# Deformable layer of a four-layer kernel: block end, first sample and one norm re-ordered

## The chip, the cores and the metric

The kernel runs on one core of a Trainium2 chip. Its engines work side by side, each through its own instructions in order: TensorE (PE) multiplies matrices, VectorE (DVE) and ScalarE (ACT) work elementwise, GpSimd (POOL) does elementwise work too, and SyncE (SP) issues most of the DMAs. The metric is the device time of one execution in microseconds (us), of which the median over several runs is given.

## The reference

The input x is fp32, 8 samples of 384 channels on a 32 x 32 image. Four layers follow each other, each as `x = x + layer(groupnorm(x))`:

```python
x = x + L0(_gn(x), ...)   # selective state-space scan (Mamba), 32 groups in _gn
x = x + L1(_gn(x), ...)   # deformable convolution, this case's main subject
x = x + L2(_gn(x), ...)   # layer norm, selective scan, MLP
x = x + L3(_gn(x), ...)   # shifts and a 5 x 5 filter per shift group
```

Layer 1 splits the channels into three groups of 128, one for each kernel size K = 3, 5, 7:

```python
def deform_block(x, ow, ob, dw, pw, pb, K):
    offsets = conv2d(x, ow, ob, K // 2)          # 2*K*K offsets per pixel
    out = deform_depthwise(x, offsets, dw, K, K // 2)
    return conv2d(out, pw, pb, 0)                # 128 -> 128, 1 x 1
...
out = jnp.concatenate([out3, out5, out7], axis=1)
return out * se_weight(out, fc1_w, fc2_w)        # squeeze and excite
```

`deform_depthwise` samples x at each tap's position plus its offset, bilinearly and with zeros outside the image, and sums over the K x K taps with one weight per channel and tap.

## The kernel before

Layer 0 and layer 2 are built by one function, in steps of two half samples; each step is a plan of units in which loads, products, scans and norms are put by hand. At the last step of layer 0 there is no next pair of samples, so `plan` puts in the norm of the deformable layer's first sample instead: `norm_load` (a DMA of x), `norm_stats` (DVE, L308), the aggregate (DVE, L146), the group mean (PE, L155), the deviations, their squares and sums, and the reciprocal root (ACT). Before the change this chain began at unit 0 of that step, as in all steps.

The deformable layer is `deform_fast`, from 2798.7 us to about 5260 us. A general version stands behind a flag for offsets out of reach. Bilinear weights are "hats": for the row distance (`hats_y`, two parts) and the column distance (`hats_x`), each an ACT absolute value and an ACT relu. DVE weighs the input cells with the tap weights (`weigh`, L1738, fxk) and multiplies the hats (`product`, L1755, fsm); PE multiplies fxk by fsm and accumulates in PSUM (`products`, L1792, wacc). Cells come from `cells_map` (DVE), `rows_pe` (PE transposes), `rows_act` (ACT), a store to DRAM (`cells_out`, fxd) and four loads that repeat them over partitions (`cells_in`, fxt8, 1 MB each). The positions (pixel plus offset) are stored (fposd) and read back repeated by `positions` (fpyx, 1 MB each).

A sample is three blocks, K = 3, 5, 7 (g = 0, 1, 2). A block is a list of units: its taps in groups of eight (four units each), and before them one single tap (two units). That makes 6, 14 and 26 units, 46 a sample. The loop in `deform_fast` runs over slots u: it issues the position load, then the work put in places act0, pe0 and dve0, then PE's unit u interleaved with DVE's unit u+1, then the hats due in this slot (y hats first), then act1, dve1 and pe1. Nothing reorders this: engines take instructions in the order issued. All tiles are rings of a fixed number of buffers, fhy 2, fhx 2, fpyx 2, fsm 6, fxk 4, fxt8 4, fw 4.

The accumulator has one buffer of five PSUM banks. So at a block's end, slot `end`, `sums_act` (act0, ACT copies fdsb<-wacc, L1474) and `sums` (dve0, L1479) empty it before PE starts the next block; `point`, `point_act` and, after K=7, the squeeze and excite follow in the next slots.

The offsets of K=3 and K=5 are direct convolutions on PE (`conv`, L1395). Those of K=7 are built from 16 pieces of short filters (`fir`, L1333), whose weights are computed once on POOL (`fir_weights`, firw), stored (fwd, on POOL's queue) and loaded piece by piece (`fir_load`, fw, on SP's queue). Pieces start five slots ahead of a sample, or three ahead for the first.

The first sample's x (xn0, tile fxn, 1.5 MB) is loaded in one DMA when layer 0 ends. Then per K: biases, a grid, weights; L1104 adds obk to the grid on POOL for K=7, and L1105 adds ob to obk on DVE for all K.

The lines of the profile that the change touches: L725 to L738 (norm), L1078 (load of xn0), L1104 and L1105, L1141 to L1152 (lead and hats), L1174 (act0), L1584 to L1589 (cells).

Of the kernel before, what the change touches and what calls it, by code (L numbers as in the profile page):

```python
# [10 lines left out]
ALU = mybir.AluOpType  # L11
# [6 lines left out]
G = C // P  # L18
# [84 lines left out]
class Net:  # L103
# [112 lines left out]
    def ssm_layer(self, li, src, dst, shift=None):  # L216
        tc, nc, ins = self.tc, self.nc, self.ins
# [4 lines left out]
        with ExitStack() as ctx:  # L222
# [455 lines left out]
            for b in range(self.nb):  # L678
                s0, s1 = {"b": b, "h": 0, "sl": slice(0, TS)}, {"b": b, "h": 1, "sl": slice(TS, L)}
# [13 lines left out]
            def plan(prev, s, nxt):  # L693
                act, dve, pool, pe = queues = [[[] for _ in range(T + NU)] for _ in range(4)]

                def put(q, t, fn, *args):
                    if not args or args[0]:
                        q[t].append((fn, *args))

                for j in range(ND):  # L700
                    t = NU * j
# [6 lines left out]
                    n, k = (s, j + 2) if j + 2 < ND else (nxt, j + 2 - ND)  # L708
# [13 lines left out]
                for t in sorted({*TG, *TS2}):  # L722
                    put(act, t, exp_ln)
                nn = nxt if nxt or mlp else {"b": 0, "h": 0, "src": dst}
                put(pe, 0, norm_load, nn)  # L725
                if nn and nn["h"] == 0:
                    put(dve, 2, norm_stats, nn, 0)
                    put(dve, 3, norm_stats, nn, 1)
                    put(dve, 3, lambda n: n.update(gn_mv=self.gn_aggr(n["gn_st"])), nn)
                    put(pe, 4, lambda n: n.update(gn_ps=self.gn_mean(n["gn_mv"])), nn)  # L730
                    put(dve, 5, lambda n: n.update(gn_grp=self.gn_dev(n["gn_mv"], n["gn_ps"])), nn)
                    put(act, 6, lambda n: n.update(gn_dm=self.gn_square(n["gn_grp"][1])), nn)
                    put(pe, 6, lambda n: n.update(gn_ps=self.gn_mean2(n["gn_dm"])), nn)
                    put(dve, 8, lambda n: n.update(gn_var=self.gn_sum(n["gn_grp"][0], n["gn_ps"])), nn)
                    to = () if nxt else self.gns[1]
                    put(act, 9, lambda n: n.update(gn=self.gn_rstd(n["gn_grp"][0], n["gn_var"], *to)), nn)
                    put(act, 9, lambda n: n["sib"].update(gn=n["gn"]), nxt)
                put(act, 10, norm_apply, nxt)  # L738
                if mlp:
# [52 lines left out]
            with tc.manual_schedule(engines=ENGINES):  # L792
# [40 lines left out]
                for i, (s, j, m) in enumerate(units):  # L833
                    c, t = divmod(i, T)
                    if t == 0:
                        queues = plan(
                            steps[c - 1] if c else None, s, steps[c + 1] if c + 1 < len(steps) else None
                        )
                        for k, q in enumerate(over or ()):
                            for i0, items in enumerate(q):  # L840
                                queues[k][i0][:0] = items
                        act, dve, pool, pe = queues
                        over = [q[T:] for q in queues]
# [228 lines left out]
    def deform_fast(self, src, dst):  # L1072
        tc, nc, ins = self.tc, self.nc, self.ins
        with ExitStack() as ctx:
            wp = ctx.enter_context(tc.tile_pool(name="w1f", bufs=1))
            self.q1 = ctx.enter_context(tc.tile_pool(name="q1", bufs=1))
            self.xn0 = self.q1.tile([P, G, L], F32, name="fxn")
            nc.sync.dma_start(out=self.xn0, in_=src(0))  # L1078
            self.fwd = self.dram.tile([P, NFIR * NFIR, 2 * 49], F32, name="fwd", bufs=1)
            with tc.tile_pool(name="fw", bufs=1) as fw:  # L1080
                self.fir_weights(fw.tile([P, NFIR, NFIR, 2 * 49], F32, name="firw"), ins["owf"])
# [4 lines left out]
            for g, K in enumerate(KS):  # L1086
                K2, (n, st, cols) = K * K, CONV[K]
                rows = 2 * K2
                queue = nc.scalar if K == 7 else nc.sync
                ow = None if n == 1 else wp.tile([P, K2, st], F32, name=f"fow{K}")  # L1090
                ob = wp.tile([P, 1], F32, name=f"fob{K}")
                obk = wp.tile([P, 1], F32, name=f"fobk{K}")
                grid = wp.tile([P, cols], F32, name=f"fgrid{K}")
                for t in (ob, obk, grid) + ((ow,) if n > 1 else ()):
                    nc.gpsimd.memset(t, 0.0)
                if n > 1:
                    queue.dma_start(out=ow[:, :, :rows], in_=ins[f"ow{K}"])
                for i in range(n):
                    r = slice(i * st, i * st + rows)
                    queue.dma_start(out=ob[r], in_=ins[f"ob{K}"])  # L1100
                    queue.dma_start(out=obk[r], in_=ins["c_cols"][:rows, Q_K + g : Q_K + g + 1])
                    queue.dma_start(out=grid[r], in_=ins["c_grid"][:rows, i * cols : (i + 1) * cols])
                if n == 1:
                    nc.gpsimd.tensor_scalar(grid[:rows], grid[:rows], obk[:rows], None, ALU.add)  # L1104
                nc.vector.tensor_tensor(obk, obk, ob, ALU.add)  # L1105
                nq = K2 // NO
                wk = wp.tile([P, nq + 1, P], F32, name=f"fwk{K}")
                for t in range(NO):
                    queue.dma_start(
                        out=wk[t::NO, :nq, :],  # L1110
                        in_=ins[f"dw{K}"][t : NO * nq : NO, :].partition_broadcast(CELL),
                    )
                queue.dma_start(out=wk[:, nq, :], in_=ins[f"dw{K}"][NO * nq, :].partition_broadcast(P))
                self.f[K] = (ow, ob, obk, grid, wk)
# [22 lines left out]
            for b in range(self.nb):  # L1137
                for g in range(G):
                    first[b, g] = len(units)
                    units += [(b, g, j, h) for j in self.order(g) for h in range(self.parts(g, j))]  # L1140
            hats, loads = {}, {}  # L1141
            for u, (b, g, j, h) in enumerate(units):
                if h == 0:
                    one = self.parts(g, j) == 2
                    lead = 4 if j == 0 else 3
                    loads[u - 5 if one or j else u - 6] = b, g, j
                    for t, fn, k in (
                        ((-3, self.hats_x, 0), (-2, self.hats_y, 0), (-1, self.hats_y, 1))
                        if one
                        else ((-lead, self.hats_x, 0), (-2, self.hats_y, 0), (-1, self.hats_y, 1), (0, self.hats_x, 1))  # L1150
                    ):
                        hats.setdefault(u + t, []).append((fn, b, g, j, k))  # L1152
            self.state = {}
            for b in range(self.nb):
                for g in range(G):
# [3 lines left out]
            def run(u, *where):  # L1159
                for place in where:  # L1160
                    for fn, *args in places.pop((u, place), ()):
                        fn(*args)

            engines = ENGINES - {mybir.EngineType.Pool}
            with tc.manual_schedule(engines=engines):
                for u in range(min(slots), max(slots) + 1):

                    def unit(i):
                        return units[i] if 0 <= i < len(units) else None

                    now, after = unit(u), unit(u + 1)
                    if u in loads:
                        self.positions(*loads[u])
                    run(u, "act0", "pe0", "dve0")  # L1174
                    if now and u == first[now[:2]]:
                        self.begin(now)
                    pe = list(self.unit_pe(*now)) if now else []
                    dve = list(self.unit_dve(*after)) if after else []
                    for k in range(max(len(pe), len(dve))):
                        for q in (pe, dve):  # L1180
                            if k < len(q):
                                q[k]()
                    for fn, *args in sorted(hats.get(u, ()), key=lambda h: h[0] == self.hats_x):
                        fn(*args)
                    run(u, "act1", "dve1", "pe1")
# [40 lines left out]
    def block_steps(self, b, g, first, put, weights, src, dst):  # L1226
        nc, K = self.nc, KS[g]
        K2, pad = K * K, K // 2
        n, st, cols = CONV[K]
        ow, ob, obk, grid, _ = self.f[K]  # L1230
# [5 lines left out]
        s0 = first[b, g]  # L1236
# [315 lines left out]
        if g == 0:  # L1552
            t = t0 - 30
# [19 lines left out]
        else:  # L1573
            t = t0 - 5 if b else t0 - 3
# [6 lines left out]
                    k += 1  # L1581
                put(t + k, "dve0" if ph > 1 else "act0", fir_take, ph)
            put(t + k, "dve0", fir_end)
        put(s0 - 5, "dve1", cells_map)  # L1584
        put(s0 - 4, "pe1", rows_pe)
        put(s0 - 3, "act0", rows_act)
        put(s0 - 3, "act0", cells_out)
        for q in range(4):
            put(s0 - 2 + q, "dve0", cells_in, q)  # L1589
        put(end, "act0", sums_act)  # L1590
        put(end, "dve0", sums)
        put(end + 1, "pe1", point)
# [544 lines left out]
```

## Time and profile before

| what | us |
|---|---|
| median of 3 runs | 8797.08 (8791.13 to 8799.9) |
| the profiled execution | 8793.49 |
| its span, first to last instruction | 8791.7 |
| deformable layer | about 2798.7 to 5260 |
| one sample of it, in the steady state | 297.3 |

The granted TensorE clock was 0.909 of full speed on average over the span. Busy time over the whole span (share and number of instructions):

```profile
PE 7389.6 (84%) x29688; PEld 3814.4 (43%) x29688; DVE 7510.6 (85%) x8477; ACT 5818.7 (66%) x9501; POOL 5571.8 (63%) x3383
```

PEld is the loading of weights into the array, which overlaps PE. No engine is full over the whole; each layer has its own limit. The slices show it (40 equal slices of the span, busy tenths):

```profile
PE   7888888788886899999999975788888888888886
...
DVE  6999999999996788988898886898898988898872
...
POOL 6999999999997000000000007999898989999954
```

In the eleven slices where POOL is at 0 the deformable layer runs: there PE is at 8 or 9 and DVE at 7 to 9.

### The profile page before, as it was taken

Reading aid. Unit: us, or ns where it says so; the run is one execution under the profiler, and the core shown is the slowest. Engines: PE = TensorE matmul, PEld = TensorE weight load, DVE = VectorE, ACT = ScalarE, POOL = GpSimd, SP = SyncE. Lnnn points to the kernel's source line nnn. Section 1 sums busy time; section 2 is a strip of 40 time slices with the busy share of each in tenths; the row PEclk is TensorE's granted clock in tenths of the full one; section 3 lists DMA queues with packets and bytes.
Section 4 is the critical chain, followed back from the end, with each engine's and each line's share of the span. In section 5 each row is a group of like instructions: output and inputs, shape, how many; then the busy total and the mean of one; then the engine's idle time right before and its main releaser. Section 6 shows DMA issues by size and latency. Waiting matters only on the chain. (4 is left out here: it accounts for less than half of the span.)

```text
span 8791.7 us, 91535 instructions
## 1 busy us (share of the span) xinstructions
PE 7389.6 (84%) x29688; PEld 3814.4 (43%) x29688; DVE 7510.6 (85%) x8477; ACT 5818.7 (66%) x9501; POOL 5571.8 (63%) x3383
## 2 busy tenths in 40 slices
PE   7888888788886899999999975788888888888886
PEld 2232233223222788788878861233333333333232
DVE  6999999999996788988898886898898988898872
ACT  6777777777774656665666556676777777776740
POOL 6999999999997000000000007999898989999954
PEclk8899899899887999999999997899889999999988
DMA  4555545555454654464446434566666656666646
GB/s 127 123 127 120 125 116 125 126 122 126 115 126 115 169 141 117 112 165 132 118 125 160 128 85 113 136 149 159 156 148 145 154 139 154 151 150 160 159 135 112
DMA packets 803572, 1179.30 MB, mean 134 GB/s; under 512 B 267042, under 2 KB 419650, under 8 KB 769288
## 3 DMA queue, kind: packets, MB, share of 16 engines
q1 hardware_dynamic: 743780, 1157.20, 53.7%
q10 hardware_dynamic: 57844, 10.06, 0.6%
q0 software_dynamic: 1456, 6.07, 0.2%
q8 instruction: 237, 3.88, 0.2%
q14 instruction: 255, 2.09, 0.1%
HBM read 984.11 MB, written 188.98 MB: 133 GB/s over the span
## 5 line engine op out<-in xcount | busy, mean ns | idle before, releaser
L539 POOL TENSOR_TENSOR db<-dub,bc 128x1024 f32<-128x1024 f32 x1536 | 3608.7, 2359 | 377.5 <-DVE hs L551 166.7
L531 ACT ACTIVATE da<-dtb,vec 128x512 f32<-128x512 f32 x3072 | 2122.1, 691 | 609.2 <-DVE hs L564 410.5
L551 DVE TENSOR_TENSOR_SCAN da<-da,db 128x1024 f32<-128x1024 f32 x960 | 2193.3, 2285 | 129.9 <-ACT da L531 86.9
L472 POOL TENSOR_TENSOR dt<-dt,sp_e 128x512 f32<-128x512 f32 x96 | 122.5, 1276 | 2473.1 <-DMA bc<-bcd 2468.8
L1792 PE MATMUL wacc<-fsm,fxk 128*128 128x195 f32 (+21 forms) x10624 | 1572.4, 306 | 132.5 <-DVE fsm L1755 69.7
L1792 PEld LDWEIGHTS wacc<-fsm,fxk 128*128 128x128 f32 x10624 | 1472.7, 195 | 269.1 <-DVE fsm L1755 141.3
L551 DVE TENSOR_TENSOR_SCAN hs<-da,db 128x1024 f32<-128x1024 f32 x576 | 1315.0, 2283 | 198.2 <-POOL db L524 86.2
L562 POOL TENSOR_TENSOR hs<-hs,bc 128x1024 f32<-128x1024 f32 x576 | 1358.0, 2358 | 33.8 <-ACT st L557 33.8
L564 DVE TENSOR_TENSOR hs<-da,bc 128x1024 f32<-128x1024 f32 x960 | 1175.5, 1224 | 127.9 <-PE y L574 78.6
L574 PE MATMUL y<-hs,cols 128*32 128x512 f32 x6144 | 975.4, 654 | 279.1 <-POOL hs L562 253.7
L1755 DVE TENSOR_TENSOR fsm<-fhy,fhx 128x585 f32<-128x585 f32 (+39 forms) x3136 | 1007.6, 383 | 92.9 <-PE wacc L1792 89.9
L1738 DVE TENSOR_TENSOR fxk<-fxt,fwk 128x1024 f32<-128x1024 f32 (+1 forms) x688 | 809.6, 1177 | 12.2 <-DMA fxt<-fxd 11.4
L1715 ACT ACTIVATE fhy<-fpyx,cell 128x416 f32<-128x416 f32 (+10 forms) x832 | 422.8, 580 | 374.7 <-DVE fsm L1755 374.6
L574 PEld LDWEIGHTS y<-hs,cols 128*32 128x32 f32 x6144 | 191.7, 114 | 1004.1 <-issue 516.1
L651 PE MATMUL ps_m<-hid,wm 128*128 128x512 f32 x1152 | 550.6, 633 | 61.8 <-ACT hid L646 27.8
L632 PE MATMUL ps_h<-t,wm 128*128 128x512 f32 x1152 | 531.1, 605 | 45.0 <-DVE sp_e L464 24.4
L1698 ACT ACTIVATE fhx<-fpyx,cell 128x352 f32<-128x352 f32 (+9 forms) x640 | 344.3, 609 | 237.0 <-DVE fsm L1755 222.8
L364 PE MATMUL ps_in<-xn,winr 128*128 128x512 f32 x576 | 326.8, 714 | 175.0 <-ACT xn L353 127.1
L651 PEld LDWEIGHTS ps_m<-hid,wm 128*128 128x128 f32 x1152 | 227.0, 203 | 394.7 <-issue 283.0
L632 PEld LDWEIGHTS ps_h<-t,wm 128*128 128x128 f32 x1152 | 216.1, 193 | 364.7 <-issue 273.4
L583 PE MATMUL ps_z<-xn,winr 128*128 128x512 f32 x576 | 303.0, 674 | 47.7 <-DVE sp_e L464 47.7
L1720 ACT ACTIVATE fhy<-fhy,cols 128x1184 f32<-128x1184 f32 (+8 forms) x208 | 307.4, 1478 | 6.8
(238 smaller groups left out, 9826.3 us busy)
## 6 DMA issues: line engine op xcount, KB each, us to landing
dtb<-dtd SPq DMA_DIRECT2D x768, 256.0 KB
dub<-dtd SPq DMA_DIRECT2D x768, 256.0 KB
fpyx<-fposd SPq DMA_DIRECT2D x104, 1024.0 KB
fxt<-fxd SPq DMA_DIRECT2D x96, 1024.0 KB
wm<-in_w SPq DMA_DIRECT2D x96, 768.0 KB
bc<-bcd SPq DMA_DIRECT2D x256, 256.0 KB
x<-x SPq DMA_DIRECT2D x73, 768.0 KB
dtd<-dt SPq DMA_DIRECT2D x192, 256.0 KB
```

Source lines behind the costliest of these rows:

```text
L531: nc.scalar.activation(da[:, i, :], s["dtb", j][:, k, :], AF.Exp, scale=na[:, j, n + i : n + i + 1])
L539: nc.gpsimd.tensor_tensor(db, du, s["bc"][p][:, 0], ALU.mult)
L551: nc.vector.tensor_tensor_scan(h1, da1, db1, 0.0, ALU.mult, ALU.add)
L562: nc.gpsimd.tensor_tensor(s["hs", m], s["hs", m], c, ALU.mult)
L564: nc.vector.tensor_tensor(hs_tile(s, m), s["da", m], c, ALU.mult)
L574: nc.tensor.matmul(s["y"][k * IP : (k + 1) * IP, :], sel, s["hs", p * NSUB + k][:, i, :], start=mlp and p == 0 and i == 0, stop=p == NQP - ...
L632: nc.tensor.matmul(ps, s["w1", q][:, k, f * P : (f + 1) * P], s["t"][:, k, :], start=(k == 0), stop=(k == G - 1))
L651: nc.tensor.matmul(ps, s["w2", q][:, f, o * P : (o + 1) * P], s["hid", q][:, f, :], start=(f == 0), stop=(f == 3))
L1715: nc.scalar.activation(hy[:, at : at + (yb - ya) * W], s["pyx", j][:, 0, ya * W : yb * W], AF.Abs, bias=bias)
L1738: nc.vector.tensor_tensor(t[:, :n], x, wk[:, j : j + 1, :].to_broadcast([P, n, P]), ALU.mult)
L1755: nc.vector.tensor_tensor(self.sub(sm, at, [(r * w, n), (w, r), (1, w)]), self.sub(hy, hy_at[by] + xa, [(r * W, n), (W, r), (1, w)]), self ...
L1792: nc.tensor.matmul(a[:, ya - 4 * o : yb - 4 * o, xa:xb], k, self.sub(sm, sm_at[by], [(w, yb - ya), (1, w)]), start=o not in s["open"], sto ...
```

## The change

There are five edits.

- In the last step of layer 0 the norm chain of the next sample is put 14 units later. In all other steps its units are as before.
- The first sample's x is loaded in three DMAs, one for each channel group.
- The DVE add of ob to obk is left out for K=7 (its obk is not read after the grid has taken it).
- The hats are re-timed. The single tap's second y hats go from the slot before the block's first unit into that slot itself, right behind act0, and so behind `sums_act` of the block before. The first x hats of the first group of eight are put 4, 5, 4 slots ahead for K = 3, 5, 7 (before: 4 for each); for K=3 the second x hats come one slot earlier. The first sample's K=3 single tap has its positions loaded 12 slots ahead instead of 5, and its group of eight has them 12 ahead instead of 6.
- The first sample's K=3 cells (`cells_map`, `rows_pe`, `rows_act`, `cells_out`, `cells_in`) are put 8 slots earlier.

```diff
--- before.py
+++ after.py
@@ -722,18 +722,19 @@
                 for t in sorted({*TG, *TS2}):
                     put(act, t, exp_ln)
                 nn = nxt if nxt or mlp else {"b": 0, "h": 0, "src": dst}
-                put(pe, 0, norm_load, nn)
+                t = 0 if nxt else 14
+                put(pe, t, norm_load, nn)
                 if nn and nn["h"] == 0:
-                    put(dve, 2, norm_stats, nn, 0)
-                    put(dve, 3, norm_stats, nn, 1)
-                    put(dve, 3, lambda n: n.update(gn_mv=self.gn_aggr(n["gn_st"])), nn)
-                    put(pe, 4, lambda n: n.update(gn_ps=self.gn_mean(n["gn_mv"])), nn)
-                    put(dve, 5, lambda n: n.update(gn_grp=self.gn_dev(n["gn_mv"], n["gn_ps"])), nn)
-                    put(act, 6, lambda n: n.update(gn_dm=self.gn_square(n["gn_grp"][1])), nn)
-                    put(pe, 6, lambda n: n.update(gn_ps=self.gn_mean2(n["gn_dm"])), nn)
-                    put(dve, 8, lambda n: n.update(gn_var=self.gn_sum(n["gn_grp"][0], n["gn_ps"])), nn)
+                    put(dve, t + 2, norm_stats, nn, 0)
+                    put(dve, t + 3, norm_stats, nn, 1)
+                    put(dve, t + 3, lambda n: n.update(gn_mv=self.gn_aggr(n["gn_st"])), nn)
+                    put(pe, t + 4, lambda n: n.update(gn_ps=self.gn_mean(n["gn_mv"])), nn)
+                    put(dve, t + 5, lambda n: n.update(gn_grp=self.gn_dev(n["gn_mv"], n["gn_ps"])), nn)
+                    put(act, t + 6, lambda n: n.update(gn_dm=self.gn_square(n["gn_grp"][1])), nn)
+                    put(pe, t + 6, lambda n: n.update(gn_ps=self.gn_mean2(n["gn_dm"])), nn)
+                    put(dve, t + 8, lambda n: n.update(gn_var=self.gn_sum(n["gn_grp"][0], n["gn_ps"])), nn)
                     to = () if nxt else self.gns[1]
-                    put(act, 9, lambda n: n.update(gn=self.gn_rstd(n["gn_grp"][0], n["gn_var"], *to)), nn)
+                    put(act, t + 9, lambda n: n.update(gn=self.gn_rstd(n["gn_grp"][0], n["gn_var"], *to)), nn)
                     put(act, 9, lambda n: n["sib"].update(gn=n["gn"]), nxt)
                 put(act, 10, norm_apply, nxt)
                 if mlp:
@@ -1075,7 +1076,8 @@
             wp = ctx.enter_context(tc.tile_pool(name="w1f", bufs=1))
             self.q1 = ctx.enter_context(tc.tile_pool(name="q1", bufs=1))
             self.xn0 = self.q1.tile([P, G, L], F32, name="fxn")
-            nc.sync.dma_start(out=self.xn0, in_=src(0))
+            for g in range(G):
+                nc.sync.dma_start(out=self.xn0[:, g, :], in_=src(0)[:, g, :])
             self.fwd = self.dram.tile([P, NFIR * NFIR, 2 * 49], F32, name="fwd", bufs=1)
             with tc.tile_pool(name="fw", bufs=1) as fw:
                 self.fir_weights(fw.tile([P, NFIR, NFIR, 2 * 49], F32, name="firw"), ins["owf"])
@@ -1102,7 +1104,8 @@
                     queue.dma_start(out=grid[r], in_=ins["c_grid"][:rows, i * cols : (i + 1) * cols])
                 if n == 1:
                     nc.gpsimd.tensor_scalar(grid[:rows], grid[:rows], obk[:rows], None, ALU.add)
-                nc.vector.tensor_tensor(obk, obk, ob, ALU.add)
+                else:
+                    nc.vector.tensor_tensor(obk, obk, ob, ALU.add)
                 nq = K2 // NO
                 wk = wp.tile([P, nq + 1, P], F32, name=f"fwk{K}")
                 for t in range(NO):
@@ -1138,18 +1141,23 @@
                 for g in range(G):
                     first[b, g] = len(units)
                     units += [(b, g, j, h) for j in self.order(g) for h in range(self.parts(g, j))]
-            hats, loads = {}, {}
+            hats, loads, single = {}, {}, {}
             for u, (b, g, j, h) in enumerate(units):
                 if h == 0:
                     one = self.parts(g, j) == 2
-                    lead = 4 if j == 0 else 3
-                    loads[u - 5 if one or j else u - 6] = b, g, j
+                    lead = (4, 5, 4)[g] if j == 0 else 3
+                    loads[u - 12 if b == g == 0 else u - 5 if one or j else u - 6] = b, g, j
                     for t, fn, k in (
-                        ((-3, self.hats_x, 0), (-2, self.hats_y, 0), (-1, self.hats_y, 1))
+                        ((-3, self.hats_x, 0), (-2, self.hats_y, 0))
                         if one
-                        else ((-lead, self.hats_x, 0), (-2, self.hats_y, 0), (-1, self.hats_y, 1), (0, self.hats_x, 1))
+                        else (
+                            (-lead, self.hats_x, 0), (-2, self.hats_y, 0), (-1, self.hats_y, 1),
+                            (-1 if g == 0 else 0, self.hats_x, 1),
+                        )
                     ):
                         hats.setdefault(u + t, []).append((fn, b, g, j, k))
+                    if one:
+                        single[u] = b, g, j
             self.state = {}
             for b in range(self.nb):
                 for g in range(G):
@@ -1171,7 +1179,10 @@
                     now, after = unit(u), unit(u + 1)
                     if u in loads:
                         self.positions(*loads[u])
-                    run(u, "act0", "pe0", "dve0")
+                    run(u, "act0")
+                    if u in single:
+                        self.hats_y(*single[u], 1)
+                    run(u, "pe0", "dve0")
                     if now and u == first[now[:2]]:
                         self.begin(now)
                     pe = list(self.unit_pe(*now)) if now else []
@@ -1581,12 +1592,13 @@
                     k += 1
                 put(t + k, "dve0" if ph > 1 else "act0", fir_take, ph)
             put(t + k, "dve0", fir_end)
-        put(s0 - 5, "dve1", cells_map)
-        put(s0 - 4, "pe1", rows_pe)
-        put(s0 - 3, "act0", rows_act)
-        put(s0 - 3, "act0", cells_out)
+        t = s0 - 5 if b or g else s0 - 13
+        put(t, "dve1", cells_map)
+        put(t + 1, "pe1", rows_pe)
+        put(t + 2, "act0", rows_act)
+        put(t + 2, "act0", cells_out)
         for q in range(4):
-            put(s0 - 2 + q, "dve0", cells_in, q)
+            put(t + 3 + q, "dve0", cells_in, q)
         put(end, "act0", sums_act)
         put(end, "dve0", sums)
         put(end + 1, "pe1", point)
```

## The prediction

> **What bounds it now.** I read in this order: the table of engines and the slices (which part is bound by what), the costliest groups for the deformable layer's lines, then the timeline at the places the diff touches, then a table of windows there. The change touches layer 0 once and the deformable layer, which runs from 2798.7 to about 5260 us. In that layer PE and DVE share the work in pairs:
>
> ```profile
> L1792 PE MATMUL wacc<-fsm,fxk 128*128 128x195 f32 (+21 forms) x10624 | 1572.4, 306 | 132.5 <-DVE fsm L1755 69.7
> L1755 DVE TENSOR_TENSOR fsm<-fhy,fhx 128x585 f32<-128x585 f32 (+39 forms) x3136 | 1007.6, 383 | 92.9 <-PE wacc L1792 89.9
> ```
>
> Each waits mostly for the other: PE in all 132.5 us, DVE 92.9. A sample takes 297.3 us and has three block ends, where the accumulator must be copied out before the next block may start. The timeline around the K=5 to K=7 end of the fourth sample (start, us, then the operation; idle before it in brackets):
>
> ```profile
> 3898.53 2.43 ACT L1698 ACTIVATE fhx<-fpyx,cell 128x352 f32<-128x352 f32 x4
> ...
> 3899.16 2.04 PE L1792 MATMUL wacc<-fsm,fxk 128*128 128x144 f32 x16 [0.49 <-DVE fsm L1755]
> ...
> 3901.00 1.84 ACT L1703 ACTIVATE fhx<-fhx,cols 128x1856 f32<-128x1856 f32 x1
> ...
> 3902.74 1.95 ACT L1715 ACTIVATE fhy<-fpyx,cell 128x384 f32<-128x384 f32 x4
> ...
> 3904.73 1.41 ACT L1720 ACTIVATE fhy<-fhy,cols 128x1344 f32<-128x1344 f32 x1
> ...
> 3906.05 1.11 ACT L1474 COPY fdsb<-wacc 128x448 f32<-128x448 f32 x3
> ...
> 3907.20 1.93 DVE L1479 TENSOR_TENSOR fdsb<-fdsb,wacc 128x320 f32<-128x320 f32 x4 [2.44 <-ACT fdsb L1474]
> ...
> 3909.28 6.98 PE L1792 MATMUL wacc<-fsm,fxk 128*128 128x288 f32 x12 [8.07 <-ACT fhy L1715]
> ```
>
> PE's last product ended at 3901.20, but ACT first finishes an x hat and makes the single tap's second y hats (3902.74 to 3906.14); DVE then idles 2.44 us and PE 8.07. The table of windows across this place (busy PE, PEld, DVE, ACT, POOL; then granted clock, DMA share, GB/s):
>
> ```profile
> 3893.00:3908.00 15.00, 7.42 (x56) 6.57 (x54) 12.53 (x30) 12.86 (x21) 0.00 (x0) 0.91 1.04 264
> 3908.00:3923.00 15.00, 13.71 (x53) 9.30 (x54) 14.97 (x32) 11.13 (x18) 0.00 (x0) 0.75 0.77 170
> ```
>
> After the gap DVE is full (14.97 of 15): DVE sets the pace, so the 2.44 us of DVE is the prize, not PE's 8.07.
>
> **Copies ahead of the y hats, K=5 end.** The copies (1.11) can start when the x hat ends, 3902.84 instead of 3906.05; they end near 3903.95. DVE is busy until about 3904.75 with norm statistics, so its sums start there instead of 3907.20: 2.45 us earlier. The y hats (3.40 us) now run 3903.95 to 3907.35; DVE, done with sums (1.93) and weighing (0.69) at 3907.3, needs them for the product that stood at 3909.65. So 2.3 to 2.45 is kept; I take 2.4. The same row (PE idle 8.06 or 8.07) stands at seven of the eight samples: 7 x 2.4 = 16.8. At the second sample PE ends its block late (3309.41, behind a norm), the y hats had time anyway, and behind the copies they come late: -0.8. **Gain 16.0.** If the hats' new place stalls as much as it frees, 0; if the statistics had room elsewhere, 3.2 each (3906.05 - 3902.84), 22.
>
> A rule weighed here: the Trainium skill, "TensorE: Matmul & The Clock Gate", Part 1, says that an idle window of about 3.4 us halves PE's clock and some 3.4 us of work restores it, and its section on oscillation prices this as throttled time times one half. The row agrees on the drop: 0.75 after a gap of 8.07, that is 15 x 0.25 = 3.75 us lost. By the rule an avoided gap would be worth 3.75 x 7 = 26 us more. By the trace it is worth nothing: the gap shrinks only to 8.07 - 2.4 = 5.7, still over the page's limit, and DVE covers the slow stretch.
>
> **The other two ends.** K=7 to the next sample's K=3:
>
> ```profile
> 4073.86 1.07 ACT L1474 COPY fdsb<-wacc 128x512 f32<-128x512 f32 x2 [2.31 <-PE wacc L1792]
> ...
> 4074.97 2.13 DVE L1479 TENSOR_TENSOR fdsb<-fdsb,wacc 128x512 f32<-128x512 f32 x3 [7.25 <-ACT fdsb L1474]
> ...
> 4076.79 3.36 PE L1333 MATMUL ps_off<-fxs,fw 128*98 128x256 f32 x16 [0.46 <-ACT ffs L1348]
> ```
>
> Here ACT waits for PE, not the reverse, and PE works through on offset filters (L1333). The copies stay where they are; the single tap's second y hats (1.12 to 1.84 + 1.28 us at L1715/L1720) now come behind them, and DVE's second product with them, 1.9 to 2.6 us later. PE wants it only after the filter piece, 0.9 to 1.6 us after DVE has it, and holds further work: cost taken as 0, from 0 to 2.6 each. The K=3 to K=5 end (ACT waits 0.92 for PE, PE never idle) alike: 0, to 1.2. The lead of the x hats and the K=3 second x hats a slot up fill ACT's waiting time (11.13 busy of 15): 0.
>
> **First sample.** Its cells_map, transposes, fxd writes and fxt8 loads go 8 slots up, its single tap's positions 7. In the order of the built program SP then issues, ahead of the first filter load (fw): four fxd (4 x 0.131 MB), two fpyx (2 x 1.05) and four fxt8 (4 x 1.05): 6.8 MB. Before, fw was first: issued 2860.62, once the fwd writes had landed (2860.56). PE runs in order, with the filter pieces 0 to 2 ahead of unit 0; its timeline:
>
> ```profile
> 2864.08 5.47 PE L1333 MATMUL ps_off<-fxss,fw 128*98 128x256 f32 x18 [3.56 <-DMA fw<-fwd]
> ...
> 2873.31 3.13 PE L1333 MATMUL ps_off<-fxq,fw 128*98 128x210 f32 x14 [1.58 <-DMA fw<-fwd]
> 2878.56 2.85 PE L1333 MATMUL ps_off<-fxq,fw 128*98 128x256 f32 x12 [2.11 <-ACT ffs L1344]
> 2881.25 3.40 PE L1792 MATMUL wacc<-fsm,fxk 128*128 128x160 f32 x16
> ...
> 2907.13 4.94 PE L1333 MATMUL ps_off<-fxs,fw 128*98 128x225 f32 x16 [2.21 <-DMA fw<-fwd]
> ```
>
> The DMA engines are full meanwhile: 304 GB/s at a share of 1.00 in 2864 to 2872, 250 GB/s on average in 2860 to 2915. So 6.8 MB cost 22.4 to 27.2 us; the middle, 24.8, puts the first filter piece at 2888.9 instead of 2864.08. PE's idle time from there to the block's end at 2915.4 was 1.58 + 2.11 + 2.21 = 5.9 us, which is won back since fxt8 and hats are then ready; from there on PE is full (34.00 of 34 in 2926 to 2960), so the rest stays: **loss 24.8 - 5.9 = 18.9.** Ends: if a third of the bytes ride free beside the fwd writes (share 0.73 in 2855 to 2864), 16.5 - 5.9 = 11; if the pieces behind also wait, 27.2. Below nothing: -5.9, if the filters come no later.
>
> The page "DMA: Bandwidth & Descriptors" of the Trainium skill speaks against this part: by "Queues, rings and completion order", descriptors of one queue are consumed in ring order, so 6.8 MB issued first do stand before fw. Its fit ("Anatomy of one DMA", stated for POOL's queue, bytes / 436 KB per us) would make them 15.6 us and the loss 9.7. I keep the trace's rate, which is of these very transfers.
>
> The three fxn loads instead of one, and the K=7 add (L1105) left out, bring the first norm forward: DVE waited 10.3 us for POOL there and PE's K=3 offsets began at 2816.9. But the K=5 offsets wait for their weights (fow, 10.8 us, to 2833) and the fwd writes for POOL's own work: 0, at most 2 either way.
>
> **Layer 0, last step.** The norm chain goes from unit 0 to unit 14. Before, PE stood 7.8 us at gn_ps (L155) for DVE's gn_mv, and DVE then idled 3.49 (for PE y) and 2.19 (for ACT dt). Later, with less queued, I take back 4 of these 5.7; ends -5.7 and +3 (the same chain blocking there). Its result is needed some 25 units later, so nothing waits.
>
> **Sum.** -16.0 + 18.9 - 4 = -1.1. Against the profiled execution (8793.5 us, span 8791.7) that is 8792.4; the median of the runs, 8797.1, lies 3.6 above it, so 8796.
>
> **Rivals.** (1) The forecast: two effects of equal size cancel, 8796; its own range, with the largest of the ends above taken alone (loss 11 instead of 18.9 and layer 0 at -5.7 below; loss 27.2 and layer 0 at +3 above), is 8786 to 8811. Chance 0.50. (2) The filters are not what sets the first block's end: fxt8 and fpyx waits (5.87 and 8.07 us long on DVE and ACT before) go and the filters come in time. Then the transition costs 0 or wins up to 5.9, and the sum is -16 - 4 - 1 = -21: 8776. For it: those waits are the longest of the stretch; against: SP's order. Chance 0.28. (3) Slower: the y hats behind the copies starve PE at the other ends. It decides once DVE's second product comes over 1.6 us late, where PE's gap of 0.46 opens by up to 2.6 at eight K=7 ends: +20.8, with the forecast's -1.1 gives 8817. For it: ACT's hats follow each other without slack there; against: PE has a filter piece to hand. Chance 0.17. (4) The order changes but frees nothing, since ACT is still held by the x hats: gain 0, +15: 8812. Chance 0.05.
>
> No change is within 0.2% (17.6 us), which is about what a measurement of this kernel can tell. Rival 2 is mostly faster; the forecast falls within for the most part; rival 3 mostly slower: faster 0.27, same 0.55, slower 0.18. A range of 8773 to 8813 leaves out rather less of rival 2 than of rival 3, two in ten in all.
>
> **What would show it.** In the new profile: the DVE idle before L1479's successor at the K=5 ends gone and PE's gap near 5.7; seven sample periods of 295 instead of 297.3; the first filter matmul near 2889 and the first block's end near 2934; gn_ps in layer 0's last step without the 7.8 us. The prediction is wrong if the first filter piece starts before 2875, or if PE shows new gaps at the K=7 ends.

## The result, and the profile after

The changed kernel takes 8794.49 us (median of 12 runs, 8788.64 to 8801.15), the kernel before 8794.94 us in 12 runs. The ratio is 1.0001, with a 95% interval from 0.9993 to 1.0009: no difference. The profiled execution's span is 8792.8 us, against 8791.7.

Behind the zero stand large parts of both signs. Landmarks that both traces have (last output matmul of layer 0, start of the first block's sums at L1479, now L1490, and end of the last block's) cut the span so:

| stretch | before | after | difference | predicted |
|---|---|---|---|---|
| start to layer 0's end | 2798.65 | 2788.87 | -9.8 | -4 |
| to the first block's sums | 120.1 | 138.4 | +18.3 | +18.9 |
| to the last block's sums | 2320.5 | 2310.6 | -9.9 | -16.0 |
| to the end | 3552.5 | 3555.0 | +2.5 | 0 |

Of the 9.8 us in layer 0, 2.7 were there before its last step began, where the code is the same: scatter. A second execution of the kernel before has 1.9 of that kind. The last row is of it too: in the other executions that stretch takes 3550.6 to 3558.0 us.

At the K=5 end of the fourth sample the timeline of the changed kernel (start, us, operation; idle before it in brackets) now reads:

```profile
3908.52 2.04 PE L1804 MATMUL wacc<-fsm,fxk 128*128 128x144 f32 x16 [0.49 <-DVE fsm L1767]
...
3910.35 1.84 ACT L1715 ACTIVATE fhx<-fhx,cols 128x1856 f32<-128x1856 f32 x1
...
3912.10 1.11 ACT L1485 COPY fdsb<-wacc 128x448 f32<-128x448 f32 x3
3912.84 1.27 DVE L1262 BATCH_NORM_STATS2 gn_st<-fxn 128x6 f32<-128x512 f32 x2
3913.09 1.98 ACT L1727 ACTIVATE fhy<-fpyx,cell 128x384 f32<-128x384 f32 x4
3914.03 1.91 DVE L1490 TENSOR_TENSOR fdsb<-fdsb,wacc 128x320 f32<-128x320 f32 x4
...
3915.11 1.42 ACT L1732 ACTIVATE fhy<-fhy,cols 128x1344 f32<-128x1344 f32 x1
...
3916.09 4.32 PE L1804 MATMUL wacc<-fsm,fxk 128*128 128x288 f32 x8 [5.53 <-DVE fdsb L1490]
```

The copies come right after the x hat, the sums follow the statistics with no idle time, and PE's gap is 5.53 instead of 8.07. The last product before the gap ends at 3910.56, and the next begins at 3916.09: a block end of this kind is 2.5 us shorter. The windows around it, placed as before (busy PE, PEld, DVE, ACT, POOL; granted clock, DMA share, GB/s):

```profile
3899.00:3914.00 15.00, 10.43 (x78) 9.25 (x76) 15.00 (x35) 9.53 (x15) 0.00 (x0) 0.95 1.02 283
3914.00:3929.00 15.00, 12.90 (x56) 9.24 (x57) 14.92 (x34) 14.79 (x23) 0.00 (x0) 0.82 1.02 222
```

DVE is full on both sides, and the clock still falls after the gap, to 0.82 where it was 0.75. The K=7 end shows what the prediction called covered:

```profile
4080.76 1.07 ACT L1485 COPY fdsb<-wacc 128x512 f32<-128x512 f32 x2 [5.03 <-PE wacc L1804]
4081.87 2.13 DVE L1490 TENSOR_TENSOR fdsb<-fdsb,wacc 128x512 f32<-128x512 f32 x3 [7.25 <-ACT fdsb L1485]
...
4083.69 3.36 PE L1344 MATMUL ps_off<-fxs,fw 128*98 128x256 f32 x16 [0.46 <-ACT ffs L1359]
...
4086.40 1.33 DVE L1767 TENSOR_TENSOR fsm<-fhy,fhs 128x512 f32<-128x512 f32 x3 [1.80 <-ACT fhy L1732]
4086.88 3.40 PE L1804 MATMUL wacc<-fsm,fxk 128*128 128x160 f32 x16
```

DVE waits 1.80 us for the moved hats, but PE's gap is 0.46 as it was, and the block takes 167.8 us as it did. It is close: DVE's product now starts 0.48 us before PE takes it, where that was 2.36.

The first sample, on PE and on SP's queue (before, SP issued the first fw at 2860.62):

```profile
2881.76 5.49 PE L1344 MATMUL ps_off<-fxss,fw 128*98 128x256 f32 x18 [30.14 <-DMA fposd<-fpos]
2887.08 5.25 PE L1344 MATMUL ps_off<-fxq,fw 128*98 128x256 f32 x24
2893.16 2.85 PE L1344 MATMUL ps_off<-fxq,fw 128*98 128x256 f32 x12 [0.83 <-ACT ffs L1355]
2895.85 3.40 PE L1804 MATMUL wacc<-fsm,fxk 128*128 128x160 f32 x16
```

```profile
2844.46 2.58 SPq L1459 DMA_DIRECT2D fxt<-fxd  x2
2861.43 0.91 SPq L1692 DMA_DIRECT2D fpyx<-fposd  x2
2862.39 1.38 SPq L1459 DMA_DIRECT2D fxt<-fxd  x2
2863.81 0.70 SPq L1334 DMA_DIRECT2D fw<-fwd  x1
```

```profile
SPq L1692 <- DMA fwd<-firw: 14.1, 3, 5.6
```

The filter load is issued behind two positions and all four cell loads. SP's queue does not keep the written order here: the single tap's position load is written a slot ahead of the fxd stores and comes behind two of the four fxt8. It also stands behind a wait for POOL's stores of fwd (the second fence: us in total, times, longest), which ends at 2861.4. The filter load was issued 3.2 us later than before, and yet PE's first filter piece begins 17.7 us later, though layer 0 ended 9.8 earlier: 92.9 us after layer 0 instead of 65.4. (The row names fposd as the releaser; the wait is for several semaphores, and the run with the filter loads first, below, shows that it is fw.)

### The profile page after: what moved, and what is told of

Read it like the earlier page. It is cut to its first block, busy times and chain, and to the rows that moved or that the text cites. A ratio compares the mean times of both kernels' runs of the same rounds, so it can differ in the third digit from the quotient of the medians.

```text
span 8792.8 us, 91545 instructions
## 1 busy us (share of the span) xinstructions
PE 7395.6 (84%) x29688; PEld 3813.9 (43%) x29688; DVE 7518.5 (86%) x8476; ACT 5814.6 (66%) x9501; POOL 5571.8 (63%) x3383
## 5 line engine op out<-in xcount | busy, mean ns | idle before, releaser
L539 POOL TENSOR_TENSOR db<-dub,bc 128x1024 f32<-128x1024 f32 x1536 | 3608.5, 2358 | 367.1 <-DVE hs L551 169.8
```

The source lines that it names most:

```text
L539: nc.gpsimd.tensor_tensor(db, du, s["bc"][p][:, 0], ALU.mult)
```

## The experiments

Each part alone, then together. "Before" in the ratios is the kernel before on the same chips.

**The norm alone** (the first hunk of the change).

> The kernel before with the norm of layer 0's last step 14 units down, and nothing else. Theory (the norm's own share is 7 us, of the 9.8 us by which layer 0 ended earlier; 2.7 us of them were there hundreds of scans before the step and are scatter between executions): from the step's first scan to the layer's end 7 us less, the layer ends near 2791.7, and the time falls by 7 us, 0.08%. Rival (the prediction's term): 4 us less. Rival 2 (the norm only shifts the wait, and what layer 0 wins the next layer waits away, since the first sample's norm or weights are late): layer 0 ends 7 us earlier, the first block of the deformable layer ends where it did, 2918.7, and the time is the same.

8788.39 against 8792.86 us, ratio 0.9995 (0.9986 to 1.0003). Layer 0's last step is 7.35 us shorter (its last scans 8.52 earlier, of which 1.16 were there before it). The prediction's 4 is too small. But from layer 0's end to the first block's sums it takes 124.3 us, 4.3 more than before, and the time alone can't tell the rest from nothing. Where the 7 us come from is seen on DVE. In the kernel before it has three waits there:

```profile
2640.03 1.22 DVE L564 TENSOR_TENSOR hs<-da,bc 128x1024 f32<-128x1024 f32 x1 [3.49 <-PE y L574]
2643.44 0.69 DVE L488 TENSOR_TENSOR sp_e<-ps_sp,u 128x512 f32<-128x512 f32 x1 [2.19 <-ACT dt L484]
...
2699.73 2.29 DVE L551 TENSOR_TENSOR_SCAN hs<-da,db 128x1024 f32<-128x1024 f32 x1 [1.83 <-POOL db L524]
```

The starts of the scans, which are the same in both kernels, tell what became of each. The step is 4.1 us ahead once the old place of the statistics is passed (3.8 of it DVE's own time for them), and 9.5 behind the first two waits. It falls back to 5.1 in the new place, where DVE does the same statistics (1.85, 1.87 and 0.34 us), and is 7.0 ahead behind the third wait. So moving the statistics is worth nothing in itself; the gain is the waits of DVE, nearly all of 3.49 and 2.19, and then the 1.83. In the new place PE waits for the same aggregate about as long as in the old one, but DVE is busy for 30.72 of 31 us around it (changed kernel; the second fence has the busy times in the order of the windows above):

```profile
2669.66 3.15 PE L155 MATMUL gn_ps<-gn_mv,gmat 128*128 128x2 f32 x14 [8.30 <-DVE gn_mv L146]
```

```profile
2661.00:2692.00 31.00, 17.97 (x75) 9.69 (x74) 30.72 (x29) 19.73 (x37) 28.29 (x21) 0.67 0.49 109
```

**A later group mean.** The norm as moved, and from the group mean on one unit later:

```diff
-                    put(pe, t + 4, lambda n: n.update(gn_ps=self.gn_mean(n["gn_mv"])), nn)
+                    v = t + 1 if t else t
+                    put(pe, v + 4, lambda n: n.update(gn_ps=self.gn_mean(n["gn_mv"])), nn)
...
```

> The norm alone 14 units down, and from its group mean on a further unit later, statistics as they were. Theory (4.3 of the 11.7 us that the first move won came back in the new place, where the matmul of the group mean stood 8.3 us on PE for the statistics): layer 0's last step 11 us shorter than before instead of 7.0 to 7.4. Rival (the wait moves on with the chain): 7 as it was.

The theory failed: its 11.7 should have been 9.6, and what came back was DVE's own time for the statistics, not PE's wait. Its rival, 7 as it was, failed too. The step is only 3.1 us shorter than before:

```profile
2669.34 3.15 PE L155 MATMUL gn_ps<-gn_mv,gmat 128*128 128x2 f32 x14 [8.31 <-DVE gn_mv L146]
2681.21 3.15 PE L166 MATMUL gn_ps<-gn_dm,gmat 128*128 128x1 f32 x14 [8.71 <-ACT gn_dm L183]
...
2689.86 1.22 DVE L564 TENSOR_TENSOR hs<-da,bc 128x1024 f32<-128x1024 f32 x1 [2.04 <-PE y L574]
2693.61 0.69 DVE L488 TENSOR_TENSOR sp_e<-ps_sp,u 128x512 f32<-128x512 f32 x1 [2.52 <-ACT dt L484]
```

PE has nothing between the two units, so the mean waits as long as before, and the second mean, now directly behind it, waits 8.71 instead of 4.73. Behind that PE is late with y, and the two waits of DVE that the move had removed are back, 4.6 us in all. This is one execution.

**The first sample's part alone** (loads of x, the K=7 add, cells and positions).

> The kernel before with the first sample's part alone: its x in three loads, the K=7 add left out, its cells 8 slots and its positions up to 7 slots earlier. Theory (the filter weights stand behind 6.8 MB on SP's queue): from layer 0's end to the end of the first block's accumulation 18 us more than before (138 against 120.1), first filter matmul some 27 us later against layer 0's end, time +18 us, +0.20%. Rival (the loss in the changed kernel comes from the hats that were re-timed, not from the loads): at most 5 us more.

8813.21 us, ratio 1.0024 (1.0014 to 1.0035), +20 us. First filter piece 94.1 us after layer 0 (+28.6), first block 140.6 (+20.5). This is the loss.

**The same, with the filter loads in front.** The changed kernel with one line different; SP then issues four fw ahead of the two fpyx and the last two fxt8:

```diff
-                    put(t + k - 3, "dve0", fir_load, k)
+                    put(t + k - 3 if b or k > 3 else s0 - 34, "dve0", fir_load, k)
```

> The changed kernel, but the first sample's first four filter loads (1.3 MB) are put ahead of the positions and of the third and fourth cell load on SP's queue; everything else as changed. Theory (the first block's end is set by when the first filter weights land, behind 4.2 MB of fpyx and fxt8): first filter matmul at 2864 to 2868 instead of 2881.8 if layer 0 ends as there, first block's end 13 to 17 us earlier than the changed kernel's 138.4 us after layer 0, time -15 us against the changed kernel, about 8779. Rival (the bytes are only moved about, the first block then waits for positions and cells instead): within 5 us of the changed kernel.

8781.75 us, ratio to before 0.9989 (0.9983 to 0.9996), where the changed kernel had 1.0001, some 10.5 us less. The first filter piece starts 17.2 us earlier than in the changed kernel, and the first block ends 10.1 earlier, below the 13 to 17 expected:

```profile
2864.06 5.58 PE L1344 MATMUL ps_off<-fxss,fw 128*98 128x256 f32 x18 [14.79 <-DMA fw<-fwd]
2869.48 5.24 PE L1344 MATMUL ps_off<-fxq,fw 128*98 128x256 f32 x24
2880.63 4.72 PE L1344 MATMUL ps_off<-fxq,fw 128*98 128x256 f32 x12 [5.90 <-ACT ffs L1355]
```

The 7 us between are in the third row: PE waits 5.90 us (0.83 in the changed kernel) for ACT to empty the filters' PSUM tile, and the piece then takes 4.72 instead of 2.85, at a granted clock of 0.56 instead of 1.00. ACT stood at the single tap's x hat for fpyx, 38.2 us, with that copy behind it.

So of the 27.5 us by which the first filter piece came later, the order of SP's loads makes 17.2. The other 10.3 (75.7 instead of 65.4 us after layer 0) are there before SP issues any fw. By the traces' semaphores POOL's last store of fwd lands 72.6 us after layer 0 here, 72.5 in the changed kernel and 70.8 with the first sample's part alone, but 61.7 to 65.5 in the ten executions without the early cells, the one with the three x loads (64.2) among them. The stores share the DMA engines with the early fxd and fxt8: while these stores were under way, the queues moved (packets, MB, share of the 16 engines) in the kernel before, 2843 to 2861,

```profile
q0 software_dynamic: 1139, 4.73, 88.8%
q1 hardware_dynamic: 108, 0.07, 1.9%
```

and in the changed kernel, 2833 to 2861.4:

```profile
q0 software_dynamic: 1200, 5.02, 61.0%
q1 hardware_dynamic: 860, 2.76, 33.3%
```

The stores are on q0, SP's loads on q1. From that landing on, the first block is no slower than elsewhere: 55.7 us here, 57.5 to 60.0 in the ten executions. So the order explains the larger part of the loss, and the late stores what is left.

**The hats alone.**

> The kernel before with the hats re-timed alone (second y hats of the single tap behind the accumulator's copies, leads 4, 5, 4, second x hats of K=3 a slot up), positions as before. Theory (seven K=5 ends at 2.5 us less DVE time each, the second sample worse by 4 to 5 us since a norm's matmul waits there for a copy that slid behind the hats): first block's end to last block's end 10 us less than before (2310 against 2320.5), PE's gap at the K=5 ends 5.5 instead of 8.07, time -10 us, -0.11%. Rival (the prediction's 16 us, and the 6 us missing in the changed kernel belong to the first sample's shift): 16 us less.

8781.44 us, ratio 0.9988 (0.9982 to 0.9995), -11.4 us. The stretch from the first to the last block's end is 11.1 us shorter (2309.4), as the theory had it.

**Only the y hats moved**, leads and the second x hats as before:

```diff
-                        ((-3, self.hats_x, 0), (-2, self.hats_y, 0), (-1, self.hats_y, 1))
+                        ((-3, self.hats_x, 0), (-2, self.hats_y, 0))
...
+                    if one:
+                        single[u] = b, g, j
...
-                    run(u, "act0", "pe0", "dve0")
+                    run(u, "act0")
+                    if u in single:
+                        self.hats_y(*single[u], 1)
+                    run(u, "pe0", "dve0")
```

> The kernel before with only the single tap's second y hats moved behind the accumulator's copies; leads and the K=3 second x hats as before. Theory (the K=5 ends win by the copies' place alone): the steady samples' K=5 end 2.5 us earlier, as with all the hats re-timed, the second sample's K=7 block 4 us longer, time -10 us. Rival (the longer lead of K=5, five slots, is part of the gain, since ScalarE otherwise still holds an x hat when PE has finished): 1 us or less at the K=5 ends.

8786.58 us, ratio 0.9988 (0.9979 to 0.9997). The fourth to sixth sample's K=5 ends come 2.53, 2.52 and 2.49 us earlier, with all hats re-timed 2.49, 2.50 and 2.50. The leads add nothing that these runs show.

**Norm and hats, without the first sample's part.**

> The changed kernel with the first sample's part undone: norm 14 units down and hats re-timed. Theory (parts add): -7 - 10 = -17 us against before, -0.19%, 8778 where before is 8795. Rival (the parts are not independent, a gain in front is waited away behind): within 5 us of before.

8775.27 us, ratio 0.9979 (0.9972 to 0.9987), -17.6 us, where -17 was expected: the parts add within the scatter (-4.5 and -11.4 measured singly).

**The second sample's K=7 block.** With the hats re-timed it takes 173.6 to 174.2 us instead of 169.8. Before, and in the changed kernel:

```profile
3323.07 1.72 PE L155 MATMUL gn_ps<-gn_mv,gmat 128*128 128x2 f32 x14 [1.09 <-ACT fog L1492]
```

```profile
3329.88 1.28 ACT L198 ACT_TABLE_LOAD   x1
...
3331.41 0.67 ACT L200 ACTIVATE gns<-gn_grp,gns 128x1 f32<-128x1 f32 x3
3331.99 0.67 ACT L1503 ACTIVATE fog<-ps_pw,pwb 128x512 f32<-128x512 f32 x1
...
3332.80 3.15 PE L155 MATMUL gn_ps<-gn_mv,gmat 128*128 128x2 f32 x14 [3.48 <-ACT fog L1503]
```

A norm's matmul waits 3.48 us for the point copy (fog) to free its PSUM, which stands behind the moved hats and a reciprocal root with two table loads. In the kernel before that wait is 1.09 (0.89 in its second execution): the root stood ahead of the copy there too, but the hats came earlier. The norm and hats version, with the root one slot later:

```diff
-                    (20, "pe0", mean2), (20, "dve1", var), (21, "act1", rstd),
+                    (20, "pe0", mean2), (20, "dve1", var), (22, "act1", rstd),
```

> Norm 14 units down and hats re-timed, as in the run without the first sample's part, and the reciprocal root of the first sample's output norm one slot later, so that its two table loads (1.28 us each) and the root no longer stand on ScalarE ahead of the K=5 block's last copies, for which a norm's matmul waits on PE. Theory (3.5 us of PE's wait there and the cold stretch behind it are the 3.8 to 4.4 us that the second sample's K=7 block became longer): that block 169.8 to 170.0 us instead of 173.6, -3.8. Rival (the block is longer by the hats' order as such): 173 and more.

That block takes 168.7 us, 4.9 less than in the same version without it, and the wait is 0.75:

```profile
3308.41 1.72 PE L155 MATMUL gn_ps<-gn_mv,gmat 128*128 128x2 f32 x14 [0.75 <-ACT fog L1501]
```

The matmuls also take 1.72 instead of 3.15 us, at a granted clock of 1.00 instead of 0.50.

> The version of the earlier look (norm 14 units down, hats re-timed, first sample as before, first output norm's root one slot later), timed. Theory (the 4.8 us of the second sample's K=7 block are real and add to the 17.6 us of the version without the later root): -22 us against before, ratio 0.9975, about 8770. Rival (the look was a low execution): -17, ratio 0.998, as without it.

8772.86 us, ratio 0.9974 (0.9964 to 0.9985): 22 us faster than before on the same chips, and the fastest version found. Its interval overlaps that of the version without the later root; the block's length in the trace, 169.8 here and 168.7 in the next run, is the better witness.

**The x loads and the add left out, on top of it.**

> The same version as the timed one, and from the first sample's part the three loads of x and the K=7 add left out, without the earlier cells and positions. Theory (the first norm comes earlier, but the first block waits for the filter weights, which the x loads don't move): first filter matmul 66 to 69 us after layer 0's end as without, time within 4 us of the timed version. Rival (the three loads shorten the start, so that fwd is written earlier, as in the changed kernel, where it was issued 47.6 us after layer 0's end instead of 46.2 and less): 3 us or more earlier.

8773.34 us, ratio 0.9976 (0.9967 to 0.9985), the same within the interval; the first filter piece comes 68.1 us after layer 0. These two edits show no effect here.

**Before once more.**

> The kernel before once more, for the scatter of its landmarks between executions. Theory (the pieces of the first sample move by some 3 us from execution to execution, since the three profiles that keep its order show 122.9, 123.5 and 124.3 us from layer 0's end to the first block's end, the first profile of before 120.1): 120 to 125 here. Rival (the re-timed hats and the later norm each cost 3 to 4 us there): 120.1 within 0.5.

One execution, 8790.65 us. From layer 0's end to the first block's sums 120.0 us, as the rival said. But the three executions of norm and hats with the same code up to there (the last two with the later root) have 122.9, 120.6 and 123.5. So some 3 us of scatter exist in this stretch. Part of it is in the last store of fwd, whose landing varies from 61.7 to 65.5 us in the ten executions without the early cells; from there to the sums they take 57.5 to 60.0. The two executions of the kernel before have the two earliest; whether the hats or the later norm also cost 1 to 4 us there stays open.

## Why the prediction was right

**That the sum is zero** was right for the reasons given, two effects of equal size: 8796 was forecast, 8794.49 came, as the forecast (1) and not one of its rivals. That it fits so closely is in part luck: the hats won 9.9 instead of 16.0 and layer 0's step 7.3 instead of 4, and these two errors largely cancel.

**First sample: right in size, and in mechanism but for one step.** Predicted +18.9, measured +18.3 in the changed kernel and +20.5 alone. The delay of the first filter piece, taken as 24.8 (22.4 to 27.2), measured 27.5 (92.9 - 65.4), and "5.9 us of idle time won back" measured 9.2; that these two errors cancel is luck. The step that is not as written is that all 6.8 MB stand ahead of fw on SP's queue. Some 2.6 MB (fxd and two fxt8) run beside POOL's stores of fwd and make these land 10.6 us later (at least 5.3 against any of the ten executions); 4.2 MB stand ahead of fw, and from the landing to the first piece it takes 20.4 us instead of 3.5. Both cost time on the same DMA engines, so the sum over the bytes came out: 5.0 MB moved in the last 20.2 us, 249 GB/s. The trace's rate was the one to take: by the fit that the Trainium skill gives ("DMA: Bandwidth & Descriptors", "Anatomy of one DMA") the loss would have been 9.7. Rival 2 falls: the first block did wait for the filters.

**K=5 ends: right in mechanism, the sum too high.** The gap of 5.53 (predicted 5.7), the 2.5 us each, and the sample of 294.9 us (predicted 295) stand in the trace. From the fourth sample on the K=5 ends give 2.52, 2.51, 2.51, 1.74 and 3.32, but the first gives 0.57 and the third 1.76, against 2.4 each. PE's gap was 8.07 at these seven, as predicted, but what DVE could win was not the same: in the third and seventh sample DVE waits 0.7 us for the load of x (fxn) that its statistics read, and the gap stays at 6.3; in the first the gap shrinks to 5.54, while the part of the block before it, at the layer's scattered start, takes 1.9 longer. With the second sample at +0.74 they sum to 14.2 instead of 16.0. Rival 4 falls.

**The step that was mis-sized: "at the second sample ... -0.8".** At its K=5 end 0.74 was lost, as predicted, but 3.93 more in the K=7 block behind it, which the prediction has at nothing. It looked for who waits for the moved hats, and not for what is queued behind them on ACT: a point copy, whose PSUM a norm's matmul needs. Moving the root away gave it back. The last sample's K=7 block, 1.65 us longer in every version with the y hats moved, is a case of the other kind: DVE waits for the moved hats there,

```profile
5096.62 1.70 DVE L1767 TENSOR_TENSOR fsm<-fhy,fhs 128x768 f32<-128x768 f32 x3 [0.78 <-ACT fhy L1732]
...
5100.14 1.75 DVE L1767 TENSOR_TENSOR fsm<-fhy,fhx 128x88 f32<-128x88 f32 x6 [0.69 <-ACT fhy L1732]
```

and keeps that delay to the block's end, so half of the 3.32 won just before is lost again.

**The other ends: right.** K=7 and K=3 ends are equal to 0.1 us in the steady samples, though DVE's product waits 1.80 us there. Rival 3 falls, by the 0.48 us that are left.

**Layer 0: too small.** "I take back 4 of these 5.7" measured 7.2 to 7.4 by the last scans, in seven executions. The reading of DVE's two idle times was right; the discount on them was not, since nearly all of it was won, and the third wait, 1.83 us for POOL, was not seen. No run separates that third one. The sign that was named, gn_ps without its 7.8 us, did not come: PE waits 8.30 in the new place, where it does not hold DVE up.

## What to carry to other kernels

When two parts of a change cancel, the total says nothing about either: cut the trace at landmarks that both kernels have, and take the parts apart, as 17.6 us lay in leaving one of them out. When loads are moved earlier on a shared queue, list everything that now stands ahead of what was first, and what now runs beside the stores that it waits for, in bytes, and price it at the rate of that stretch. When an instruction is moved behind another on an in-order engine, look at what is queued behind it there and whose buffer that frees.

## What was not expected of the hardware

In the steady state the block times of different executions of the same code agree to about 0.1 us, while the start of the same layer, where PE waits for DMAs, scatters by 3 us. Loads on one queue delayed the stores on another by 5 to 11 us, with both on the same DMA engines. On ACT, a root with two table loads of 1.28 us each, with hats moved in front of it, idled PE for 3.5 us; the 14 small matmuls behind took 3.15 instead of 1.72 us, at half the granted clock.
